# Loads of layer 1 issued by ScalarE instead of SyncE, with the first pass's row loads and normalisation spread over a strip

## The chip, the cores and the metric

The kernel runs on one core of a Trainium2 chip. The time is the device time of one execution in microseconds (us); it is 20,884.65 us as the median of three runs before the change (20,843.57 to 20,913.25). The engines are called as in the profile: PE (TensorE, matmuls; PEld is its weight load), DVE (VectorE), ACT (ScalarE), POOL (GpSimd), SP (SyncE, which here only issues DMAs). A name with a q (SPq, ACTq) is the instruction queue that issues DMAs. All data are 32-bit floats.

## The reference, cut to what matters

Four images of 48 channels and 256x256 pixels go through four residual layers, each `x = x + layer_n(norm(x))`, where `norm` takes mean and variance over groups of channels of an image. The change lies in layer 1 alone:

```
h = einsum('oc,bchw->bohw', w_in, norm(x))        # 48 -> 288 channels, 1x1
h = irfft2(rfft2(8x8 patches of h) * fft_mask)    # per channel a filter on each patch
h = conv3x3(h, depthwise, zero padding)           # per channel, across patch edges
x = x + einsum('oc,bchw->bohw', w_out, gelu(h[:144]) * h[144:])   # 144 -> 48
```

Layer 0 is of a like kind (Fourier products of patches), layer 2 samples an integral image at learned places (indirect DMAs on POOL), layer 3 is a gated network with a patch filter.

## The kernel before, in words

**Two streams.** The program is written as two generators whose steps are interleaved by due time: stream a runs layers 0 and 1 for image after image and then layer 3; stream b runs the first statistics, the weights of layer 1's filters (`patch_weights`) and layer 2. Each `yield n` adds n to the stream's own clock, and the stream that is behind goes next. So layer 1 of image 0 runs with nothing beside it, and layer 1 of images 1 to 3 runs beside layer 2 of the image before. `self.dma` (L227) issues on SP for stream a and on POOL for stream b; the column loads of layer 2 (`A<-x`, `B<-x`) are issued by ACT. A scheduler then puts the instructions of each engine in an order of its own, keeping the dependences, and buffers are handed out by pools (`hs`, `hg`, `ct` have two, `tt` three). PSUM gives stream a five banks (`self.bank()`). A DMA's landing is told by a completion semaphore; eight of them serve the DMAs of SP and ACT in turn.

**Layer 1, pass 1** (L690 to L710). An image is 16 strips of 16 rows (two halves of 8 rows, on partitions 0 to 47 and 64 to 111). `normalise(s)` takes a strip in four quarters of two rows: two loads (one for each half, 48 partitions x 516 floats, 96.8 KB) into one of two tiles `xn`, and a `tensor_scalar` on DVE (L684) that subtracts the mean, scales, and puts the rows as 8x8 patches into one of two tiles `xp`. The strip itself is 16 blocks b of two matmuls (L697, one for each half h): the block's pixels are the stationary operand, the weights `win` the moving one, and 288 channels come out in PSUM. The copy to the strip's tile `hs` is ACT's for h = 0 (L704) and DVE's for h = 1 (L702). After block 7 the whole of `normalise(s + 1)` is written. After block 15 one DMA writes `hs` (4,608 KB) to the scratch `hD` in HBM.

**Layer 1, pass 2** (L755 to L789). The 288 channels are 72 groups of four: c = 0, 1 of the gelu half, c = 2, 3 of the factor half. `fetch(g)` issues four loads: `hg` (1,024 KB, the group's patches from `hD`), `ct` (256 KB, the filter matrices), `tt` (256 KB) and `ht` (104 KB), the matrices of the 3x3 convolution within a patch and from the ring of pixels around it. Group g has four filter matmuls (L728), whose results are copied to `ys` by ACT (L734, even c) and DVE (L732, odd c). Eight DMAs (the list `AROUND`) then move the patches' edges from `ys` to the neighbours' ring `yh`. One group later `gated` takes the convolution as two matmuls for each c, from `ys` and `tt` (L741) and from `yh` and `ht` (L742), gelu on ACT (L745) and the product on DVE (L746) into `gt`; every second group one DMA writes `gt` to the scratch `gD` (1,024 KB). `fetch(g + 1)` is written ahead of group g's matmuls.

**Layer 1, pass 3** reads `gD` strip by strip, transposes and projects; the change doesn't touch it.

Of the kernel before, what the change touches and what calls it, by code (L numbers as in the profile page):

```python
# [11 lines left out]
ALU = mybir.AluOpType  # L12
# [7 lines left out]
NS = 16  # L20
# [6 lines left out]
NG = 72  # L27
# [12 lines left out]
NH = 52  # L40
# [148 lines left out]
class Net:  # L189
# [28 lines left out]
    def load(self, name, shape, pool=None):  # L218
        t = (pool or self.const).tile(shape, F32, name=name + "_sb", tag=name + "_sb")
        self.dma(t[:], self.a[name])  # L220
        return t
# [437 lines left out]
    def layer1(self, x, mr, y):  # L659
        nc, a = self.nc, self.a  # L660

        hD = self.dram.tile([128, NG, NS, 128], F32, name=self.nm("hD"))[:]
        gD = self.dram.tile([128, NS, NG // 2, 128], F32, name=self.nm("gD"))[:]
        with ExitStack() as ctx:
            w = ctx.enter_context(self.pool("wa", 1))
            sb = ctx.enter_context(self.pool("ba", 2))

            win = w.tile([112, 288], F32, name="win")
            mh = w.tile([112, 2], F32, name="mh")
            xns = [w.tile([112, 2, PW], F32, name=self.nm("xn")) for _ in range(2)]  # L670
            xps = [w.tile([112, 16, 128], F32, name=self.nm("xp")) for _ in range(2)]
            for t in xns:
                nc.vector.memset(t[32:64], 0.0)
            nc.vector.memset(mh[32:64], 0.0)
            for h in range(2):
                self.dma(win[64 * h : 64 * h + 48], a["L1_w_in"])
                self.dma(mh[64 * h : 64 * h + 48], mr[48 * h : 48 * h + 48])

            def normalise(s):

                for r in range(0, 8, 2):
                    xn = xns[r // 2 % 2]
                    self.load_rows(xn, x, 8 * s + r, 2, 64)
                    nc.vector.tensor_scalar(  # L684
                        xps[s % 2][:].rearrange("p b (r c) -> p r b c", c=16)[:, r : r + 2],
                        xn[:, :, 1:257].rearrange("p r (b c) -> p r b c", c=16),
                        mh[:, 0:1], mh[:, 1:2], ALU.subtract, ALU.mult,
                    )

            normalise(0)  # L690
            for s in range(NS):
                xp = xps[s % 2]
                hs = sb.tile([128, 4 * NG, 2, 16], F32, name="hs", tag="hs")
                for b in range(16):
                    for h in range(2):
                        ps = self.bank()
                        nc.tensor.matmul(  # L697
                            ps[:, :288], xp[64 * h : 64 * h + 48, b, :], win[64 * h : 64 * h + 48],
                            start=True, stop=True,
                        )  # L700
                        if h:
                            nc.vector.tensor_copy(hs[:, :, h, b], ps[:, :288])  # L702
                        else:
                            nc.scalar.copy(hs[:, :, h, b], ps[:, :288])  # L704
                    if b == 7:
                        if s + 1 < NS:
                            normalise(s + 1)
                        yield 13
                self.dma(hD[:, :, s, :], hs[:].rearrange("p (g c) h b -> p g (c h b)", c=4))
                yield 13  # L710
        with ExitStack() as ctx:
            w = ctx.enter_context(self.pool("wb", 1))
            sb = ctx.enter_context(self.pool("bb", 2))
            ys = [w.tile([128, YL], F32, name=self.nm("ys")) for _ in range(2)]
            yhs = [w.tile([NZ, YL], F32, name=self.nm("yh")) for _ in range(2)]
            hts = [w.tile([NZ, 4, 128], F32, name=self.nm("ht")) for _ in range(3)]
            for t in ys + yhs + hts:
                nc.vector.memset(t[:], 0.0)

            pick = lambda t, k, c: t[:k, Y0 + YC * c : Y0 + YC * c + 32 * YW].rearrange(  # L720
                "p (h s b) -> p s h b", h=2, b=YW
            )[:, :, :, :16]
            order = lambda t: t.rearrange("p (s h b) -> p s h b", h=2, b=16)
            todo, gt = None, None

            def filtered(c):
                ps = self.bank()
                nc.tensor.matmul(  # L728
                    ps[:].rearrange("p (s n) -> p s n", n=32), ct[:, c, :], hg[:, :, c, :], start=True, stop=True
                )  # L730
                if c % 2:
                    nc.vector.tensor_copy(pick(yt, 128, c), order(ps[:]))  # L732
                else:
                    nc.scalar.copy(pick(yt, 128, c), order(ps[:]))  # L734

            def gated(c):
                go, yo, yho, to, ho = todo
                both = []
                for q in (c, c + 2):
                    ps = self.bank()  # L740
                    nc.tensor.matmul(order(ps[:]), to[:, q, :], pick(yo, 128, q), start=True, stop=False)  # L741
                    nc.tensor.matmul(order(ps[:]), ho[:, q, :], pick(yho, NZ, q), start=False, stop=True)  # L742
                    both.append(ps)
                gl = sb.tile([128, 512], F32, name="gl", tag="gl")
                nc.scalar.activation(gl[:], both[0][:], AF.Gelu)  # L745
                nc.vector.tensor_mul(  # L746
                    gt[:, :, 2 * (go % 2) + c, :], gl[:].rearrange("p (s n) -> p s n", n=32),
                    both[1][:].rearrange("p (s n) -> p s n", n=32),
                )


            def fetch(g):
                hg = sb.tile([128, NS, 4, 32], F32, name="hg", tag="hg")
                self.dma(hg[:].rearrange("p s c n -> p s (c n)"), hD[:, g])
                ct = sb.tile([128, 4, 128], F32, name="ct", tag="ct")  # L755
                self.dma(ct[:], self.cD[g])
                tt = sb.tile([128, 4, 128], F32, name="tt", tag="tt", bufs=3)
                ht = hts[g % 3]
                tv = self.tD[4 * g : 4 * g + 4].rearrange("c (k m) -> k c m", m=128)
                self.dma(tt[:], tv[:128])  # L760
                self.dma(ht[:NH], tv[128:])
                return hg, ct, tt, ht

            fetched = {0: fetch(0)}
            for g in range(NG + 1):
                if g < NG:
                    yt = ys[g % 2]
                    if g + 1 < NG:
                        fetched[g + 1] = fetch(g + 1)
                    hg, ct, tt, ht = fetched.pop(g)  # L770
                if todo is not None and todo[0] % 2 == 0:
                    gt = sb.tile([128, NS, 4, 32], F32, name="gt", tag="gt")
                for c in range(2):
                    if g < NG:
                        filtered(2 * c)
                        filtered(2 * c + 1)
                    if todo is not None:
                        gated(c)
                if g < NG:
                    yh = yhs[g % 2]  # L780
                    n = YL - 2 * Y0
                    for k, m, p0, dp, far in AROUND:
                        self.dma(
                            yh[k : k + m, Y0 : Y0 + n], yt[p0 : p0 + (m - 1) * dp + 1 : dp, Y0 + far : Y0 + far + n]
                        )
                if todo is not None and todo[0] % 2:
                    self.dma(gD[:, :, todo[0] // 2, :], gt[:].rearrange("p s c n -> p s (c n)"))
                todo = (g, yt, yh, tt, ht)
                yield 12  # L789
# [582 lines left out]
```

## Time and profile before

| | |
|---|---|
| median of three runs | 20,884.65 us (20,843.57 to 20,913.25) |
| profiled execution, its own time | 20,882.08 us |
| its span in the profile | 20,880.3 us, mean granted TensorE clock 0.922 |
| busy: PE, DVE, POOL, ACT | 18,892.3, 10,763.0, 8,637.2, 5,909.3 us |
| chain of work that ended last | PE 65%, DMA 15%, DVE 7%, POOL 7%, "issue" 4%, SPq 1%, ACT 1% |
| pass 1 of images 0, 1, 2, 3 | 343, 543, 543, 542 us |
| pass 2 of images 0, 1, 2, 3 | 875, 1,142, 1,149, 1,130 us |
| pass 3 of images 0, 1, 2, 3 | 277, 280, 280, 279 us |

The stages are windows of the profiled execution: pass 1 from 1983, 5699, 9901 and 14107 us, pass 2 from 2351, 6269, 10471 and 14676 us. In a row of the costliest groups, the numbers behind the bar are the group's busy time, the mean of one instruction in ns, the idle time of the engine just before the group's instructions, and what ended most of that idle time. In a timeline a row is a start, a length, the engine and line, and in brackets the idle time before it with its releaser; a DMA row on SPq or ACTq is the time that its issue took, not the transfer.

### The profile page before, as it was taken

To read this page: it belongs to the slowest core of one execution; us is meant where nothing else is said; L and a number is where in the kernel's file an instruction comes from. 1 tells how busy PE (TensorE), PEld (TensorE's weight loads), DVE (VectorE), ACT (ScalarE), POOL (GpSimd) and SP (SyncE) were. 2 spreads that over 40 slices of the span, in tenths; PEclk is the share of its full clock that TensorE was granted. 3 is DMA by queue.
4 is the path that set the end of the run, shared out by engine and by line. 5 is a ranking of instruction groups with operands and counts; after the bars stand their busy time and mean duration, and the time that the engine had idled before them with its cause. 6 is when DMAs were issued, how large, how long until landed. Compare 5 with 4: busy or idle time off the path is not lost.

```text
span 20880.3 us, 231985 instructions
## 1 busy us (share of the span) xinstructions
PE 18892.3 (90%) x79032; PEld 12001.4 (57%) x79032; DVE 10763.0 (52%) x21931; ACT 5909.3 (28%) x12275; POOL 8637.2 (41%) x8887
## 2 busy tenths in 40 slices
PE   7998798999878989998788899997888999999999
PEld 4565435666533346665433466654334787878888
DVE  4544322477765534677645447776554255555521
ACT  2333312344321123443311234433112211111111
POOL 1000000277754511777555216775552066666600
PEclk9899799999968999999689899996899999999999
DMA  4623886555588975555889755558897566666633
GB/s 114 135 55 82 233 217 194 137 132 134 132 235 230 241 207 139 130 134 127 233 230 240 219 133 130 133 127 229 236 239 225 137 150 151 158 152 160 151 76 74
DMA packets 2444896, 3440.27 MB, mean 165 GB/s; under 512 B 580102, under 2 KB 1997038, under 8 KB 2333179
## 3 DMA queue, kind: packets, MB, share of 16 engines
q1 hardware_dynamic: 1908216, 2084.50, 38.2%
q0 software_dynamic: 452560, 1110.45, 21.1%
q10 hardware_dynamic: 82944, 230.48, 4.4%
q8 instruction: 635, 10.40, 0.2%
q14 instruction: 541, 4.43, 0.1%
HBM read 2486.99 MB, written 802.77 MB: 158 GB/s over the span
## 4 chain that ended last, share of the span: by engine, by line
PE 65%; DMA 15%; DVE 7%; POOL 7%; issue 4%; SPq 1%; ACT 1%; DVEq 0%; ACTq 0%; POOLq 0%
PE ps L427 19%; POOL V L1037 7%; PE ps L947 6%; PE ps L728 5%; PE ps L435 4%; PE ps L741 4%; DMA ct<-cD 4%; PE ps L742 3%; PE ps L697 3%; PE ps L828 3%; DMA hD<-hs 2%; PE ps L1188 2%; DVE V L1050 2%; PE ps L815 1%; PE ps L966 1%
## 5 line engine op out<-in xcount | busy, mean ns | idle before, releaser
L1037 POOL DMA_INDIRECT V<-t,idx x8192 | 8227.0, 1004 | 4897.9 <-issue 2346.8
L427 PE MATMUL ps<-W,A 128*128 128x288 f32 (+1 forms) x24576 | 5547.3, 374 | 85.9 <-DMA A<-x 23.4
L427 PEld LDWEIGHTS ps<-W,A 128*128 128x128 f32 x24576 | 4281.6, 191 | 1226.6 <-issue 523.4
L227 POOL DMA_DIRECT2D X<-x x192 | 144.5, 757 | 4302.6 <-DMA x<-xt 3040.1
L1050 DVE TENSOR_TENSOR V<-V 128x1536 f32<-128x1536 f32 (+3 forms) x2048 | 1839.3, 900 | 19.2
L1048 DVE TENSOR_TENSOR V<-V,w 128x3072 f32<-128x3072 f32 x512 | 1713.3, 3346 | 35.9 <-DMA V<-t,idx 27.0
L728 PE MATMUL ps<-hg,ct 128*128 128x512 f32 x2304 | 1264.4, 676 | 417.5 <-DMA ct<-cD 339.5
L947 PE MATMUL ps<-A,W 112*96 112x512 f32 x3072 | 1544.9, 642 | 26.2 <-DVE xt L1069 21.5
L697 PE MATMUL ps<-win,xp 48*128 48x288 f32 x4096 | 1054.8, 594 | 547.9 <-DVE xp L684 232.4
L508 ACT COPY qkv<-ps 128x288 f32<-128x288 f32 x2048 | 769.9, 400 | 2641.1 <-PE ps L427 1258.4
L435 PE MATMUL ps<-W,B 58*128 58x288 f32 (+1 forms) x8192 | 1271.5, 391 | 26.1 <-DMA B<-x 13.8
L742 PE MATMUL ps<-yh,ht 65*128 65x512 f32 x2304 | 1163.1, 649 | 145.7 <-DMA yh<-ys 111.6
L531 DVE BATCH_NORM_STATS2 bs<-ps 128x6 f32<-128x96 f32 x2048 | 397.4, 251 | 1634.3 <-PE ps L529 1632.3
L741 PE MATMUL ps<-ys,tt 128*128 128x512 f32 x2304 | 1174.1, 632 | 27.6 <-DVE ys L732 25.7
L697 PEld LDWEIGHTS ps<-win,xp 48*128 48x128 f32 x4096 | 647.3, 259 | 924.3 <-ACT hs L704 291.9
L1168 DVE TENSOR_TENSOR gp<-gl,ps 128x192 f32<-128x192 f32 x1024 | 353.8, 351 | 1588.1 <-ACT gl L1167 1579.9
L728 PEld LDWEIGHTS ps<-hg,ct 128*128 128x128 f32 x2304 | 468.0, 211 | 1051.6 <-issue 949.1
L1167 ACT ACTIVATE gl<-ps 128x192 f32<-128x192 f32 x1024 | 332.7, 330 | 2529.4 <-PE ps L427 2245.4
L435 PEld LDWEIGHTS ps<-W,B 58*128 58x128 f32 x8192 | 762.4, 186 | 454.1 <-issue 346.4
L746 DVE TENSOR_TENSOR gt<-gl,ps 128x512 f32<-128x512 f32 x576 | 395.1, 687 | 1142.2 <-PE ps L742 1136.6
L947 PEld LDWEIGHTS ps<-A,W 112*96 112x96 f32 x3072 | 513.9, 176 | 731.4 <-issue 690.3
L742 PEld LDWEIGHTS ps<-yh,ht 65*128 65x128 f32 x2304 | 451.3, 199 | 794.3 <-issue 699.4
(186 smaller groups left out, 24654.4 us busy)
## 6 DMA issues: line engine op xcount, KB each, us to landing
hD<-hs SPq DMA_DIRECT2D x64, 4608.0 KB
hg<-hD SPq DMA_DIRECT2D x288, 1024.0 KB
gD<-gt SPq DMA_DIRECT2D x144, 1024.0 KB
gs<-gD SPq DMA_DIRECT2D x64, 2304.0 KB
V<-t,idx POOLq DMA_INDIRECT x8192
A<-x SPq DMA_DIRECT2D x512, 193.5 KB
xt<-x SPq DMA_DIRECT2D x256, 387.0 KB
A<-x ACTq DMA_DIRECT2D x512, 193.5 KB
```

Source lines behind the costliest of these rows:

```text
L427: nc.tensor.matmul(to(q, b), A[:, r + q, 128 * b + g : 128 * b + g + 128], W[:, g, :], start=b == 0 and g == 0, stop=b == 1 and g == 2,)
L435: nc.tensor.matmul(to(q, b), B[p, r // 2, 128 * b : 128 * b + 128], W[p, 3, :], start=b == 1, stop=b == 0)
L508: nc.scalar.copy(t.qkv[:, 2 * q + b, :], banks[2 * b + q][:, 0:288])
L697: nc.tensor.matmul(ps[:, :288], xp[64 * h : 64 * h + 48, b, :], win[64 * h : 64 * h + 48], start=True, stop=True,)
L728: nc.tensor.matmul(ps[:].rearrange("p (s n) -> p s n", n=32), ct[:, c, :], hg[:, :, c, :], start=True, stop=True)
L741: nc.tensor.matmul(order(ps[:]), to[:, q, :], pick(yo, 128, q), start=True, stop=False)
L742: nc.tensor.matmul(order(ps[:]), ho[:, q, :], pick(yho, NZ, q), start=False, stop=True)
L828: nc.tensor.matmul(pp[:CP, :], pr[:, q, :], got[q][:], start=q == 0, stop=q == 2)
L947: m = nc.tensor.matmul(ps[:96, :].rearrange("p (r c) -> p r c", c=256), W[: kk[g], g, :], of[: kk[g]], start=g == 0, stop=g == 3,)
L1037: nc.gpsimd.indirect_dma_start(out=V[:, k, 4 * cr : 4 * cr + 4, :].rearrange("p e c -> p (e c)"), out_offset=None, in_=table, in_offset=ba ...
L1048: self.pinned(nc.vector.tensor_mul(Vm, Vm, wm.unsqueeze(2).to_broadcast([128, 64, 48])))
L1050: nc.vector.tensor_add(V[:, :, 0:n, :], V[:, :, 0:n, :], V[:, :, n : 2 * n, :])
```

## The change

In pass 1 the row loads are issued by ACT (`nc.scalar.dma_start`), and `normalise` is split into `load(s, n)` and `normalise(s, n)` for a quarter n. For the first strip the four pairs are written one after the other. For the others, the eight steps are written behind blocks 2, 4, 6, 7, 8, 9, 11 and 13 of the strip before, in the order of `plan`. In pass 2 the four loads of `fetch` are issued by ACT, and `fetch(g + 1)` is written behind group g's matmuls and gates (ahead of the `AROUND` DMAs) instead of ahead of them. The DMAs of `hD`, `AROUND` and `gD` stay on SP. From the end of the new lines on, line numbers of the changed kernel are 5 or 6 higher.

```
-            def normalise(s):
-
-                for r in range(0, 8, 2):
-                    xn = xns[r // 2 % 2]
-                    self.load_rows(xn, x, 8 * s + r, 2, 64)
-                    nc.vector.tensor_scalar(
-                        xps[s % 2][:].rearrange("p b (r c) -> p r b c", c=16)[:, r : r + 2],
-                        xn[:, :, 1:257].rearrange("p r (b c) -> p r b c", c=16),
-                        mh[:, 0:1], mh[:, 1:2], ALU.subtract, ALU.mult,
-                    )
-
-            normalise(0)
+
+            def load(s, n):
+                for h in range(2):
+                    nc.scalar.dma_start(xns[n % 2][64 * h : 64 * h + 48], self.rows(x, 128 * h + 8 * s + 2 * n, 2))
+
+            def normalise(s, n):
+                nc.vector.tensor_scalar(
+                    xps[s % 2][:].rearrange("p b (r c) -> p r b c", c=16)[:, 2 * n : 2 * n + 2],
+                    xns[n % 2][:, :, 1:257].rearrange("p r (b c) -> p r b c", c=16),
+                    mh[:, 0:1], mh[:, 1:2], ALU.subtract, ALU.mult,
+                )
+
+            for n in range(4):
+                load(0, n)
+                normalise(0, n)
+            plan = {2: (load, 0), 4: (load, 1), 6: (normalise, 0), 7: (load, 2), 8: (normalise, 1), 9: (load, 3),
+                    11: (normalise, 2), 13: (normalise, 3)}
...
+                    if b in plan and s + 1 < NS:
+                        do, n = plan[b]
+                        do(s + 1, n)
                     if b == 7:
-                        if s + 1 < NS:
-                            normalise(s + 1)
                         yield 13
...
             def fetch(g):
                 hg = sb.tile([128, NS, 4, 32], F32, name="hg", tag="hg")
-                self.dma(hg[:].rearrange("p s c n -> p s (c n)"), hD[:, g])
+                nc.scalar.dma_start(hg[:].rearrange("p s c n -> p s (c n)"), hD[:, g])
                 ct = sb.tile([128, 4, 128], F32, name="ct", tag="ct")
-                self.dma(ct[:], self.cD[g])
+                nc.scalar.dma_start(ct[:], self.cD[g])
...
-                self.dma(tt[:], tv[:128])
-                self.dma(ht[:NH], tv[128:])
+                nc.scalar.dma_start(tt[:], tv[:128])
+                nc.scalar.dma_start(ht[:NH], tv[128:])
...
             for g in range(NG + 1):
                 if g < NG:
                     yt = ys[g % 2]
-                    if g + 1 < NG:
-                        fetched[g + 1] = fetch(g + 1)
                     hg, ct, tt, ht = fetched.pop(g)
...
                     if todo is not None:
                         gated(c)
+                if g + 1 < NG:
+                    fetched[g + 1] = fetch(g + 1)
                 if g < NG:
                     yh = yhs[g % 2]
```

## The prediction

> **What bounds the kernel now.** I read the page's engine shares first, then its costliest groups for what PE (TensorE) waits for, then the windows by stage, and last the timeline inside one strip and one group.
>
> ```profile
> PE 18892.3 (90%) x79032; PEld 12001.4 (57%) x79032; DVE 10763.0 (52%) x21931; ACT 5909.3 (28%) x12275; POOL 8637.2 (41%) x8887
> ...
> L728 PE MATMUL ps<-hg,ct 128*128 128x512 f32 x2304 | 1264.4, 676 | 417.5 <-DMA ct<-cD 339.5
> ...
> L697 PE MATMUL ps<-win,xp 48*128 48x288 f32 x4096 | 1054.8, 594 | 547.9 <-DVE xp L684 232.4
> ...
> L742 PE MATMUL ps<-yh,ht 65*128 65x512 f32 x2304 | 1163.1, 649 | 145.7 <-DMA yh<-ys 111.6
> ```
>
> PE is busy 90% of the span, 1,988 us are idle, and the three matmul lines that the change feeds have 417.5 + 547.9 + 145.7 = 1,111 us of idle time ahead of them. The windows put that time in place; columns are length, busy PE, PEld, DVE, ACT, POOL, granted clock, DMA share, GB/s. The four lines are pass 1 and pass 2 of image 0, then of image 1.
>
> ```profile
> 1983.00:2326.00 343.00, 205.88 (x1024) 158.56 (x1024) 181.67 (x315) 153.35 (x256) 0.00 (x0) 0.67 0.86 240
> 2351.00:3226.00 875.00, 810.67 (x1701) 338.16 (x1702) 199.71 (x288) 171.62 (x285) 0.00 (x0) 0.93 0.80 216
> ...
> 5699.00:6242.00 543.00, 410.41 (x1360) 225.30 (x1360) 352.37 (x617) 170.09 (x276) 296.62 (x308) 0.64 0.80 229
> 6269.00:7411.00 1142.00, 1004.51 (x2317) 428.04 (x2317) 591.34 (x880) 192.55 (x317) 599.13 (x633) 0.90 0.91 237
> ```
>
> PE is idle 137 and 133 us in the two pass 1, 64 and 137 us in the two pass 2; images 2 and 3 repeat image 1 (132, 132; 145, 139). All of it: 1,019 us. But the DMA engines are busy 0.80 to 0.91 there. A stage can't become shorter than the larger of busy PE and DMA share x length: 295, 811, 434 and 1,039 us. So at most 48 + 64 + 3 x 109 + 320 = 759 us can be won. Why PE waits in pass 1 is seen in one strip's timeline (start, length, what; idle before in brackets):
>
> ```profile
> 2130.84 0.52 SPq L227 DMA_DIRECT2D hD<-hs  x1
> ...
> 2131.55 14.62 SPq L227 DMA_DIRECT2D xn<-x  x1
> ...
> 2133.47 1.81 PE L697 MATMUL ps<-win,xp 48*128 48x288 f32 x6 [11.00 <-DVE xp L684]
> ```
>
> SP issues the strip's hD write, and the next xn load, right behind it, takes 14.62 us to issue. The rows land late, L684 normalises late, and PE stands 11.00 us. In pass 2 SP's order is the matter:
>
> ```profile
> 2804.46 0.60 SPq L227 DMA_DIRECT2D gD<-gt  x1
> ...
> 2805.16 1.83 SPq L227 DMA_DIRECT2D hg<-hD  x1
> ...
> 2809.73 9.00 SPq L227 DMA_DIRECT2D yh<-ys  x8
> ...
> 2814.66 1.95 PE L728 MATMUL ps<-hg,ct 128*128 128x512 f32 x4 [2.28 <-DMA ct<-cD]
> ```
>
> The loads of the next group go out after the previous group's eight yh issues (9.0 us) and gD, some 9 us after their buffer was free in image 0 and 13.6 us in images 1 to 3; the filter matmul then waits 2.28 us.
>
> **What the Trainium skill says.** "DMA: Bandwidth & Descriptors", section Issuing engines are not separate DMA queues: starting DMAs from several engines saves only the sequencer's issuing time, "which is usually small". The trace disagrees on small: 14.62 us behind hD. Section Queues, rings and completion order of that page: each issuing engine has a ring of its own and the DMA engines go round between rings. So a load issued by ACT needn't stand behind hD's descriptors. The trace agrees as far as it shows it: ACT's A<-x issues take 0.3 to 1.5 us while an hD backlog lies on SP (5970 to 5976 us). Section Anatomy of one DMA: a wait on a semaphore is spent on the issuing sequencer. Here that means ACT, which has copies and gelus queued behind its loads. The waits by SP's queue show the same on SP: "<- DMA hD<-hs: 373.5" us in 22 times.
>
> **The change, part by part.** Only ACT and SP change in number: 1,664 DMAs (512 xn; 288 each of hg, ct, tt, ht) go from SP to ACT; POOL's queue, PE and DVE keep their counts. ACT's issuing time is 1,664 x 0.3 to 1.8 us; per group 1.83 + 1.17 + 0.60 + 0.59 = 4.2 us beside 172 / 73 = 2.4 us of work in a period of 12.0. That lies beside PE's work, 0 on the path as long as five PSUM banks cover a copy that stands behind one issue; without that cover up to 0.5 us a group.
>
> What counts is the wait before an issue. The built program hands eight completion semaphores in turn to all DMAs of SP and ACT, so each waits for the one eight places before it in program order. A strip of pass 1 has eight loads and one hD: nine. In image 0, in the built order, each strip's eighth load waits on ACT for hD of the strip before, and stands ahead of the ninth of ACT's 16 hs copies (L704). That wait was SP's before; now eight copies, and behind them PE through its banks, stand behind it. In images 1 to 3 the layer 2 column loads, already on ACT, shift the turn: such a wait falls ahead of copy 5 to 11 in 8 of 15 strips, and twice per image at a strip's end.
>
> *Pass 1, image 0.* The wait for xn goes (loads are issued a strip ahead). The period becomes hD's flight (18.3 to 19.3 us in this stage; estimate 20.7 with seven loads beside it), 0.5 us for the load, seven copies at PE's slow pace there (0.96 us a block: 6.7 us), 0.7 us to the next hD: 28.6 us against 22.55 (hD issues from 2017.24 to 2310.40, 13 strips). 13 x 6 = **+78 us**. Bounds: -48 (DMA floor above) to +110.
>
> *Pass 1, images 1 to 3.* A strip takes 34.5 us; copy 9 comes some 17 us after hD, whose flight is 22.2 us in the mean. Half of the strips wait some 5 us, the others no longer wait for SP: the chain gives hD 26.7% (145 us) and xn 7.7% (42 us) of this stage. I take -20 us each, **-60**; bounds -109 and +50 each.
>
> *Pass 2, image 0.* hg is issued when its buffer is free, so ct's wait ends, and SP's yh issues no longer stand behind 2805.16 to 2809.73. Late next is yh: c3's copy ends 2807.76, and 9.0 us of issues and 2 us of flight give 2818.8 against a next use at 2808.66 + 12.0 = 2820.7; but yh's semaphores now wait for hg, ct and ht of the group after next, which eats part of that lead. I take 12.0 to 11.3 us a group (PE alone: 811 / 73 = 11.1): **-50**; bounds -64 and +25.
>
> *Pass 2, images 1 to 3.* 1142 / 73 = 15.65 us, PE alone 13.8, DMA alone 0.91 x 15.65 = 14.2. With loads begun earlier the engines fill gaps, but transfers stay queued: 15.25, **-30 each, -90**; bounds -107 and +40 each.
>
> Sum: 78 - 60 - 50 - 90 = -122. The profiled execution took 20,882.08 us (span 20,880.3), 2.6 below the median of 20,884.65; 20,884.65 - 122 = **20,763 us**.
>
> **The rivals.** *A, the forecast (0.45)*: SP's backlog and lag are gone, part is paid back as hD's wait on ACT. Own range 20,640 to 20,870. *B, the large gain (0.20)*: ACT's wait for hD is covered by banks and by layer 2's PE work, and half of the 759 us comes: some 20,500. For it: PE waits on xn and ct in every strip and group. Against: in image 0 nothing else is there to do. *C, slower (0.22)*: ACT, held in order by landings, becomes the bound. It decides once hD lands later than ACT reaches the load ahead of copy 9: 18.3 us against 8 x 0.96 = 7.7 us in image 0 (certain there), 22.2 against 17 in images 1 to 3 (marginal). Price: +78, +1 us x 15 strips x 3 = +45, and in pass 2 tt and ht, waiting on ACT for yh or gD ahead of gelus, +0.5 us x 216 groups = +108: 21,115. *D, nothing (0.13)*: the change doesn't do what it says, because the DMA engines at 0.80 to 0.91 and the window of eight DMAs set both passes: 20,885.
>
> **How the numbers follow.** A measurement of this kernel can tell some 0.3%, 63 us, from no change: 20,822 to 20,947. Faster: 0.40 of A and B, 0.60. Same: 0.05 of A and 0.12 of D, 0.17. Slower: C and 0.01 of D, 0.23. From 20,500 (half of B lies below) to 21,000 (half of C above) no more than 0.2 is left out.
>
> **What would show it.** In the changed profile: L684's wait for xn (408.0 us) below 100; L728's wait for ct (339.5) below 100; the hs copies of ACT with some 13 waits of about 10 us for hD or xn in image 0; SP's wait for hD gone; the four windows near 421, 825, 523 and 1,112 us. I am wrong if pass 1 of image 0 is shorter than 343 us (no wait on ACT), if pass 2 is longer than before, or if PE waits for hs copies in images 1 to 3 more than the 270 us (151.3 by DVE, 118.8 by ACT) that L697 shows.

## The result, and the profile after

The changed kernel takes **21,721.69 us** (median of four runs, 21,703.06 to 21,728.49) against 20,886.03 us before: ratio 1.0401, 95% interval 1.0382 to 1.042. It is slower by 836 us; the forecast was 20,763, a gain. The profiled execution has a span of 21,701.0 us, 820.7 more than before. The page's rows that answer to those shown of before:

```profile
PE 19440.8 (90%) x79032; PEld 12205.1 (56%) x79032; DVE 10746.7 (50%) x21931; ACT 5915.1 (27%) x12275; POOL 8615.4 (40%) x8887
...
L748 PE MATMUL ps<-yh,ht 65*128 65x512 f32 x2304 | 1513.0, 816 | 725.1 <-DMA yh<-ys 526.9
...
L702 PE MATMUL ps<-win,xp 48*128 48x288 f32 x4096 | 1175.3, 627 | 532.4 <-ACT hs L709 382.6
...
L734 PE MATMUL ps<-hg,ct 128*128 128x512 f32 x2304 | 1231.7, 639 | 179.7 <-DMA ct<-cD 61.5
```

The wait that was aimed at did go: ct ends 61.5 us of the filter matmul's idle time instead of 339.5. In its place the ring's matmul (L748, L742 before) waits 526.9 us for `yh`, instead of 111.6. In pass 1 the wait for `xp` has become one for ACT's copies (382.6 us). The windows, same columns as before: pass 1 and pass 2 of image 0, then of image 1.

```profile
1983.00:2368.00 385.00, 260.25 (x1024) 191.19 (x1024) 181.39 (x317) 158.20 (x256) 0.00 (x0) 0.57 0.72 213
2394.00:3466.00 1072.00, 922.10 (x1701) 377.71 (x1702) 200.32 (x289) 171.73 (x285) 0.00 (x0) 0.84 0.63 177
5932.00:6495.00 563.00, 437.49 (x1360) 232.89 (x1360) 350.79 (x616) 169.15 (x276) 304.97 (x316) 0.63 0.76 223
6522.00:7828.00 1306.00, 1088.19 (x2318) 455.06 (x2319) 589.12 (x881) 192.51 (x317) 596.07 (x630) 0.83 0.80 207
```

By the first and last matmul of each stage (in pass 2, of its filter matmuls), pass 1 is longer by 41, 21, 14 and 20 us and pass 2 by 197, 163, 168 and 202 us: 95 + 729 = 824, all of the difference. Pass 3 has changed by 3 us at most. The DMA engines are less busy than before (0.63 for 0.80, 0.80 for 0.91), so it isn't bandwidth. In pass 2 of image 0 PE now stands ahead of the gates (L748) and hardly anywhere else: 35 times, 146 us in all.

```profile
PE ps L748 <- DMA tt<-tD: 92.3, 22, 4.7
PE ps L748 <- DMA yh<-ys: 50.0, 12, 5.6
PE ps L734 <- DMA ct<-cD: 30.3, 2, 26.6
PE ps L748 <- issue: 3.7, 1, 3.7
```

In these rows the numbers are us in all, times, and the longest. The waits by SP's queue in the same stage say where the lateness comes from; first before, then after:

```profile
SPq L227 <- DVE ys L732: 60.5, 36, 5.7
SPq L227 <- DMA tt<-tD: 48.5, 43, 2.2
SPq L227 <- PE ps L741: 45.6, 70, 1.7
SPq L227 <- DMA hg<-hD: 38.9, 34, 1.9
```

```profile
SPq L227 <- DMA hg<-hD: 331.4, 70, 7.8
SPq L227 <- DMA yh<-ys: 126.4, 97, 3.4
SPq L227 <- DMA ht<-tD: 96.4, 37, 5.9
```

SP no longer issues the loads, yet it waits for them more than before: 70 times 4.7 us for the landing of `hg`. What it has to issue then are the eight `AROUND` DMAs of a group, called the halo here. The reason lies in the built program: the eight completion semaphores are handed out in program order over both queues, and a DMA waits for the last one that held its semaphore. The trace's records of DMA issues carry the number: SP and ACT share semaphores 108 to 115, POOL has 99 to 106. With the loads on SP, each stood in SP's order behind the halo DMAs of the group before. On ACT they are begun right after the group's last copy, so their place in the turn is ahead of, and in the midst of, that group's own halo DMAs. A stretch of the changed kernel's timeline in pass 2 of image 0:

```profile
2898.25 27.27 SPq L227 DMA_DIRECT2D yh<-ys  x16
...
2899.95 6.81 PE L748 MATMUL ps<-yh,ht 65*128 65x512 f32 x8 [4.27 <-DMA tt<-tD]
...
2913.07 0.33 ACTq L760 DMA_DIRECT2D hg<-hD  x1
...
2915.51 3.73 PE L748 MATMUL ps<-yh,ht 65*128 65x512 f32 x8
...
2919.43 0.33 ACTq L767 DMA_DIRECT2D ht<-tD  x1
...
2930.28 4.74 PE L748 MATMUL ps<-yh,ht 65*128 65x512 f32 x6 [4.04 <-DMA tt<-tD]
```

Sixteen halo DMAs, two groups' worth, took 27.27 us to issue, 13.6 for a group's eight, against 9.00 before. (A group's gates are four matmuls in the program and eight records here.) The single issues and landings in the trace show what the second eight waited for:

- The first halo DMA has the semaphore of `hg`. `hg` was begun at 2913.07, when its buffer was free, and landed at 2917.83; the halo DMA went out at 2917.91.
- The sixth and seventh have the semaphores of the second and third, because the loads have used up places of the turn. They went out at 2922.82 and 2924.04, 0.02 us after those had landed.
- The eighth has that of `ht`, whose buffer is free only after the gates of the group before (2915.51 and 3.73 us). `ht` was begun at 2919.43 and landed at 2924.39, in time for the eighth at 2924.80.
- The eighth landed at 2930.04, and the next gates start at 2930.28. It was 5.2 us in flight, beside `hg` and `ct` of the next group (begun at 2923.64 and 2923.99). The eighth of the group before, without such company, took 2.0 (2909.74 to 2911.78).

The tag "DMA tt<-tD" on the last row names another transfer that landed then; in the program L748 waits for the eight halo DMAs.

The stage alternates. In every second group PE waits at the gates, 4.1 us in the mean, and the steps are those above: of 34 such groups the first halo DMA was held by `hg` in 33, a later one by its own group's landings in 33, the eighth by `ht` in 3. In the groups between, `ht` does hold the seventh halo DMA (in 33 of 36), but the gates find their halo in place, because PE is slow there: after the pause eight records of L748 took 6.81 us, without one 3.73. A period that ends in a wait is 14.9 us in the mean and one without it 15.3, where PE's busy time before was 811 / 73 = 11.1 a group.

It is still a loop, over two groups: gates that start late, PE's matmuls behind them, the buffer that they free, `hg`, the halo, gates.

### The profile page after: what moved, and what is told of

Its sections match the earlier page's. It is cut to its first block, busy times and chain, and to the rows that moved or that the text cites. A ratio compares the mean times of both kernels' runs of the same rounds, so it can differ in the third digit from the quotient of the medians.

```text
span 21701.0 us, 230822 instructions
## 1 busy us (share of the span) xinstructions
PE 19440.8 (90%) x79032; PEld 12205.1 (56%) x79032; DVE 10746.7 (50%) x21931; ACT 5915.1 (27%) x12275; POOL 8615.4 (40%) x8887
## 3 DMA queue, kind: packets, MB, share of 16 engines
q1 hardware_dynamic: 1576792, 1550.02, 28.6%
## 4 chain that ended last, share of the span: by engine, by line
PE 66%; DMA 17%; DVE 6%; POOL 6%; issue 3%; ACT 1%; SPq 1%; ACTq 0%; DVEq 0%; POOLq 0%
PE ps L427 20%; PE ps L953 6%; PE ps L748 6%; POOL V L1043 6%; PE ps L435 4%; DMA hD<-hs 4%; DMA yh<-ys 4%; PE ps L734 3%; PE ps L747 3%; PE ps L834 3%; PE ps L702 2%; PE ps L1194 2%; DMA tt<-tD 2%; PE ps L891 1%; DVE V L1056 1%
## 5 line engine op out<-in xcount | busy, mean ns | idle before, releaser
L748 PE MATMUL ps<-yh,ht 65*128 65x512 f32 x2304 | 1513.0, 816 | 725.1 <-DMA yh<-ys 526.9
L702 PE MATMUL ps<-win,xp 48*128 48x288 f32 x4096 | 1175.3, 627 | 532.4 <-ACT hs L709 382.6
L953 PE MATMUL ps<-A,W 112*96 112x512 f32 x3072 | 1626.2, 671 | 10.3 <-DVE xt L1075 5.6
L748 PEld LDWEIGHTS ps<-yh,ht 65*128 65x128 f32 x2304 | 556.3, 248 | 1552.3 <-issue 1214.7
L734 PE MATMUL ps<-hg,ct 128*128 128x512 f32 x2304 | 1231.7, 639 | 179.7 <-DMA ct<-cD 61.5
L702 PEld LDWEIGHTS ps<-win,xp 48*128 48x128 f32 x4096 | 698.2, 273 | 972.4 <-ACT hs L709 607.7
L740 ACT COPY ys<-ps 128x512 f32<-128x512 f32 x576 | 347.2, 603 | 3021.1 <-PE ps L734 1619.2
```

Source lines behind the costliest of these rows:

```text
L702: nc.tensor.matmul(ps[:, :288], xp[64 * h : 64 * h + 48, b, :], win[64 * h : 64 * h + 48], start=True, stop=True,)
L734: nc.tensor.matmul(ps[:].rearrange("p (s n) -> p s n", n=32), ct[:, c, :], hg[:, :, c, :], start=True, stop=True)
L953: m = nc.tensor.matmul(ps[:96, :].rearrange("p (r c) -> p r c", c=256), W[: kk[g], g, :], of[: kk[g]], start=g == 0, stop=g == 3,)
```

## The experiments

Two theories stood against the **loop** (halo DMAs held by the landing of later loads): **contention** (loads now fly beside the halo DMAs and slow them) and **ACT's blocked queue** (rival C). The runs come from several chips. On three of them every kernel, the one before included, takes 25.0 to 25.7 ms, with longer stages where layer 2 runs beside; why is open. Image 0's stages agree across all chips (before's pass 1: 340 to 343 us), so stage times are compared in image 0 or on one chip.

**p1only**: the change's pass 1, the pass 2 of before.

> The change's pass 1 with the pass 2 of before. If the two passes lose time each for itself: the 95 us that the windows of pass 1 show (41 + 21 + 14 + 20) stay and pass 2 is as before, some 20,980 us, windows near 384, 563, 556, 562 and 875, 1142, 1149, 1130. If pass 1's new loads are what slows pass 2 (clock or queue carried over), pass 2 keeps part of its 729 us: 21,200 or more.

Measured: 20,972.02 us, ratio 1.0043 (1.0029 to 1.0058). Pass 1 took 385, 554, 558 and 560 us; pass 2 took 866, 1,133, 1,123 and 1,130.

**p2only**: the pass 1 of before, the change's pass 2.

> The pass 1 of before with the change's pass 2. If the passes are independent: 20,885 + 729 = some 21,615 us, pass 2 near 1072, 1305, 1316, 1331. If they are not, the loss is well below 700 us.

Measured: 21,619.93 us, ratio 1.0355 (1.0334 to 1.0376); pass 2 took 1,066, 1,323, 1,327 and 1,318 us, pass 1 as before. The two losses nearly add up: 78 us of p1only and 726 of p2only make 803 of the 836. No run moves `fetch` in the source alone, with its DMAs on SP; that this part changes nothing is not shown. With the halo on POOL it makes no difference where `fetch` stands (p2_yh_pool and best, below: 790 and 789 us).

**p2_hg**: on top of p2only, ct, tt and ht back on SP; hg stays on ACT.

```
-                nc.scalar.dma_start(ct[:], self.cD[g])
+                self.dma(ct[:], self.cD[g])
...
```

> Pass 1 of before; in pass 2 only hg is issued by ACT, ct, tt and ht stay on SP. Loop theory (the halo DMAs wait, through the completion semaphores, for the landing of ct, tt and ht of a later group; ht waits for the gates before): the loop is cut, since these three again stand behind the halo DMAs in SP's order, and pass 2 is near before or better: 840 to 890 us in image 0, 1,100 to 1,150 in the others. Contention theory (hg, 1 MB, now flies beside the halo DMAs and slows them): most of the loss stays, over 1,000 and over 1,250. Theory of ACT's blocked queue: a quarter of the issues, a quarter of the loss: 920 and 1,185.

Measured: ratio 1.0218 (1.0197 to 1.0239); pass 2 took 1,052, 1,234, 1,217 and 1,225 us. My own number for the loop theory (840 to 890) failed. The waits of SP's queue in image 0 show how:

```profile
SPq L227 <- DMA hg<-hD: 320.6, 36, 11.2
SPq L227 <- PE ps L742: 22.8, 15, 4.7
```

In this order `ht` shares hg's semaphore and stands on SP ahead of a group's halo DMAs, so half of the groups wait some 9 us for `hg`. The wait has moved by one DMA and the halo is held all the same. In images 1 to 3 about half of the loss has gone. By itself image 0's time (over 1,000) would also fit contention.

**p2_yh_pool**: on top of p2only, the halo on POOL, whose DMAs have semaphores of their own.

```
-                        self.dma(
+                        nc.gpsimd.dma_start(
                             yh[k : k + m, Y0 : Y0 + n], yt[p0 : p0 + (m - 1) * dp + 1 : dp, Y0 + far : Y0 + far + n]
```

> Pass 1 of before; pass 2 of the change, but the eight halo DMAs are issued by POOL, whose DMAs have completion semaphores of their own. To be read in image 0, where POOL has no other work (in images 1 to 3 they stand behind gathers). Loop theory: yh no longer waits for the landing of loads, pass 2 of image 0 goes from 1,072 to 860 to 930 us. Contention theory and the theory of ACT's blocked queue: it stays over 1,030.

Measured: ratio 1.0249 (1.0225 to 1.0273) for the whole, but **790 us** in image 0's pass 2, below before's 875.

```profile
2349.00:3139.00 790.00, 768.59 (x1700) 321.82 (x1701) 200.00 (x288) 171.75 (x285) 295.69 (x568) 0.98 1.02 240
```

```profile
2806.13 0.33 ACTq L754 DMA_DIRECT2D hg<-hD  x1
...
2807.41 4.17 POOL L783 DMA_DIRECT2D yh<-ys  x8 [4.26 <-issue]
...
2808.57 3.73 PE L742 MATMUL ps<-yh,ht 65*128 65x512 f32 x8
```

The first fence is the window of the stage, the second its timeline: the eight halo DMAs go out in 4.17 us right beside `hg`. They take 7.8 to 9.4 us to land, and cost nothing. PE is busy 97% at a granted clock of 0.98. SP's queue still waits for `hg`, but only `gD` stands behind that wait:

```profile
SPq L227 <- DMA hg<-hD: 442.6, 34, 44.2
```

So loads that fly beside the halo don't make the loss by themselves, and neither does ACT's issuing of them. By the issue records, ACT's loads waited 102 us in this stage, nearly all for PE to free a buffer. In the change it was 146 us, 27 of them for landings, most of them of ACT's own `tt`. That holds for image 0. The run gives the halo other semaphores, another queue and a shorter issue (4.17 us for eight) at once; that the semaphores held it is read from SP's waits, not separated by this run. In images 1 to 3 the halo shares POOL with layer 2's gathers: its first DMA went out 4.1 to 4.4 us after the group's last copy in the mean, against 0.6 in image 0, and pass 2 took 1,326 to 1,334 us, as in p2only.

**p2_nocorner** and **b_nocorner**: the change's pass 2, and the kernel before, each with four of the eight halo DMAs left out.

```
-                    for k, m, p0, dp, far in AROUND:
+                    for k, m, p0, dp, far in AROUND[:4]:
```

> Pass 1 of before, pass 2 of the change, with the four one-partition corner DMAs of the halo left out (their part of the result is not computed): four loads and four halo DMAs a group, so that the eight semaphores come round once a group and a halo DMA waits for DMAs of the group before, not for loads begun after its own data were ready. If the turn of the semaphores makes the loop, it is gone in all four images: 790 to 850 and 1,050 to 1,140 us. If it is ACT's blocked queue or the contention of loads and halo, most of the loss stays: over 1,000 and over 1,250.

> The kernel before with the same four corner DMAs left out, as the yardstick of the run above: four issues of 0.75 us less on SP for each group. 840 to 870 us in image 0 and 1,080 to 1,140 in the others if SP's issue order is what delays ct there; unchanged if the engines' share (0.91) is.

Measured (one chip): p2_nocorner 938.7 us in image 0 and 1,288, 1,287, 1,287 in the others; b_nocorner 821.1 and 1,289, 1,323, 1,294. The number for image 0 (790 to 850) failed, and so did the rivals' (over 1,000): with gD in the turn it doesn't come round evenly, and SP still waits 190.3 us for `hg` in image 0. The two go together: the wait fell from 331.4 to 190.3 us (by 43%) and the loss from 197 to 939 - 821 = 118 us (by 40%). In images 1 to 3 the times are over the rivals' 1,250, but so are the yardstick's: no loss is left against it, though ACT issues every load. On such a chip there is less to lose, as the next pair shows. b_nocorner itself is 54 us below before's 875 in image 0, more than expected: the halo cost time in the kernel before too.

**p2_noht** and **p2only_b** (one chip): the loads of `ht` taken out, and the yardstick.

```
-                nc.scalar.dma_start(ht[:NH], tv[128:])
+                if g < 3:
+                    nc.scalar.dma_start(ht[:NH], tv[128:])
```

> Pass 1 of before, pass 2 of the change, but ht is loaded for the first three groups alone and those matrices are used for all (the ring's part of the convolution is computed with wrong matrices). It takes one edge out of the loop: gates of the group before -> ht begun by ACT -> landing -> eighth halo DMA -> landing -> gates. The other edge, first halo DMA waits for hg's landing, stays. If the ht edge closes the loop of 14.9 us a group: 840 to 940 us in image 0. If hg's landing alone does: over 1,030.

> The change's pass 2 with the pass 1 of before once more, as the yardstick on the chip of the run beside it: 1,066 us in image 0, as before. In images 1 to 3, if this chip is one where layer 2's gathers run slower and pass 2 of before takes 1,360 to 1,420: the loop theory says that the loop is not lengthened by that, so the loss against before is smaller than 163 to 201 us; if the loss is a slowed engine or contention, it is as large or larger.

Measured: 1,005 us for p2_noht, 1,069 for p2only_b in image 0. Neither number of the expectation was met: leaving out `ht` is worth 64 of some 195 us, a third. It also takes one DMA out of each group's turn, and in the change `ht` held the halo mostly in groups whose gates didn't wait, so the third can't be put down to the ht edge alone.

SP's waits in the first 937 us of that stage:

```profile
SPq L227 <- DMA hg<-hD: 399.9, 65, 10.8
SPq L227 <- DMA gD<-gt: 49.2, 32, 2.4
```

SP's wait for `hg` is still 399.9 us there. That the larger part of the loss is the first halo DMA, and SP's queue behind it, held until `hg` has landed, fits this; no run has that edge alone taken out. In images 1 to 3 p2only_b took 1,421, 1,415 and 1,422 us, p2_noht 1,371, 1,355 and 1,361, 49 to 60 us less. How much p2only_b loses there is seen from the totals on that chip: 25,664.95 us against 25,375.82 before (ratio 1.0112, 1.0083 to 1.0142), 289 us. Image 0's pass 2 accounts for some 200 of them (1,069 against 866 to 875 elsewhere), which leaves some 30 us for each other image (an estimate; 4 to 54 by the interval), and not 163 to 202: where the stage is slow for another reason, the loop is mostly covered.

**p1_3rows** and **p1_3rows_sp**: pass 1 with seven DMAs a strip instead of nine, issued by ACT or by SP; pass 2 of before.

```
-            xns = [w.tile([112, 2, PW], F32, name=self.nm("xn")) for _ in range(2)]
+            xns = [w.tile([112, 3, PW], F32, name=self.nm("xn")) for _ in range(2)]
...
+            ROWS = (3, 3, 2)
...
+            plan = {2: (load, 0), 4: (load, 1), 6: (normalise, 0), 7: (load, 2), 9: (normalise, 1), 12: (normalise, 2)}
```

> The change's pass 1 (loads by ACT), but a strip is loaded in three pieces of 3, 3 and 2 rows instead of four of 2: six loads and one hD make seven DMAs a strip for eight semaphores, so in image 0 no load waits for hD any more. Pass 2 as before. If hD's wait on ACT, ahead of the ninth copy, makes pass 1 of image 0 longer: its 384 us fall below before's 343, to 300 to 335 (DMA share 0.86 x 343 = 295). If the early loads themselves do it (they fly beside hD), it stays at 375 or more. Images 1 to 3 keep some of these waits through layer 2's column loads: 530 to 560 each.

> As the run with three pieces, but the loads are issued by SP, spread over the strip as in the change. If the issuing engine is what matters in images 1 to 3 (a wait on SP holds only DMAs, one on ACT holds copies): 520 to 540 us each, below the ACT version. In image 0, SP issues the loads behind hD's descriptors again (14.6 us in one case): near the ACT version if the loads go out ahead of hD, else 330 to 345.

Measured: ratios 0.9967 (0.9955 to 0.9979) and 0.9978 (0.9967 to 0.999). Image 0's pass 1 takes 290.9 us with ACT, below the 300 to 335 expected, and 361.1 with SP, above its 330 to 345; before 343.4, the change 384.4. The change's wait in this stage, a case of it in the timeline, and the window of p1_3rows:

```profile
ACT hs L709 <- DMA hD<-hs: 119.5, 14, 9.9
```

```profile
2122.93 0.31 ACTq L682 DMA_DIRECT2D xn<-x  x1
2123.28 1.63 ACT L709 COPY hs<-ps 128x288 f32<-128x288 f32 x3 [8.50 <-DMA hD<-hs]
```

```profile
1983.00:2274.00 291.00, 241.44 (x1024) 182.76 (x1024) 179.74 (x301) 159.21 (x256) 0.00 (x0) 0.64 0.95 280
```

The load at 2122.93 waits for hD (issued 2104.5) on ACT, and the ninth copy behind it starts 8.50 us late. With seven DMAs on eight semaphores ACT's waits for hD shrink from 119.5 us to 18.8, and the DMA engines are 0.95 busy. That the pieces are fewer and larger is not enough: with SP they are the same, and there L689 waits 148.8 us for xn, as L684 does in the kernel before. In images 1 to 3 the order turns round: 645, 643, 641 us with ACT and 621, 633, 617 with SP, where the pass 1 of before took 637 to 660 on that chip: ACT is the worse place there; that it is because copies stand behind a held load, and layer 2's column loads take part in the turn, is argued from the order and not shown by a run.

**best** and **c_halo0**: put together from these runs. The loads of pass 1 come in three pieces as above; c_halo0 has the first and the last edit alone.

```
+        alone = x is self.x[0]
...
+                    (nc.scalar.dma_start if alone else self.dma)(
+                        xns[n % 2][64 * h : 64 * h + 48, : ROWS[n]], self.rows(x, 128 * h + 8 * s + 3 * n, ROWS[n])
+                    )
...
+                start = nc.scalar.dma_start if alone else self.dma
+                start(hg[:].rearrange("p s c n -> p s (c n)"), hD[:, g])
...
-                        self.dma(
+                        (nc.gpsimd.dma_start if alone else self.dma)(
                             yh[k : k + m, Y0 : Y0 + n], yt[p0 : p0 + (m - 1) * dp + 1 : dp, Y0 + far : Y0 + far + n]
```

> A version put together from the runs: image 0 (nothing beside it) has the loads of pass 1 in three pieces on ACT, the fetch of pass 2 on ACT and the halo DMAs on POOL; images 1 to 3 have the loads of pass 1 in three pieces on SP, spread over the strip, and the pass 2 of before. If the gains add up: 52 (pass 1, image 0: 291 for 343) + 85 (pass 2, image 0: 790 for 875) + 3 x 15 to 28 (pass 1, images 1 to 3) = 180 to 220 us less than before, ratio 0.989 to 0.992. If the gains in images 1 to 3 belong to the slower chip alone: 137 us, 0.9935.

> The kernel before, with only the halo DMAs of image 0 issued by POOL; the fetch stays on SP. If in the run with halo on POOL the separation of halo and loads is the whole gain, whichever engine issues the loads: pass 2 of image 0 near 790, some 85 us less than before. If the early loads from ACT are needed for it: 830 to 860, and 15 to 45 us less.

Measured: best 25,438.79 us against 25,674.92 before on that chip, 236 us less, ratio **0.9905** (0.9887 to 0.9922); c_halo0 ratio 0.9968 (0.9947 to 0.9989). Image 0's pass 2 is 789 us in both, so putting the halo on POOL is the whole gain there, and which engine issues the loads then doesn't matter. It takes the halo out of the loads' turn and its issues off SP, ahead of the loads, at once; which of the two helps the kernel before is not separated. Image 0's pass 1 in best is 291 us; images 1 to 3 take 632, 632 and 627 in pass 1, against 659, 663 and 655 in c_halo0, whose pass 1 is that of before: 27 to 31 us an image, where 15 to 28 were expected. Best is faster than before on one chip; the change, measured on another, is slower than before by a ratio of 1.0401.

## Why the prediction was wrong

- **What bounds the kernel** held: PE's waits in the two passes were for xn and ct, and both shrank: ct's to 61.5 us, below 100 as said, L685's for xn from 408.0 to 212.5, which is not below 100. SP's wait for hD went from 373.5 to 21.5 us, as said.
- **Pass 2, image 0** (-50 forecast, +197 measured) is the step that failed, and images 1 to 3 (-90 forecast, +532 measured) with it. The prediction saw the wait, "yh's semaphores now wait for hg, ct and ht of the group after next", and priced it as "part of that lead" of 2 us. It should have been followed as a chain: hg's flight of 4.8 us ahead of the first halo DMA, the issues of the later ones held by landings in their own group, and the eighth's flight of 5.2 us, where 2 were counted, ahead of the gates. In place of 11.3 us a group the measured period is 14.9: PE waits 4.1 us for the halo in every second group, and in the other its matmuls take longer, which the prediction had put at nothing.
- **Rival C** was the right side with, in image 0, the wrong queue. It put the price on ACT (0.5 us a group for tt and ht, waiting for yh or gD ahead of gelus; 21,115 us). ACT's four loads waited for yh or gD only 3 us in all there, and 3 to 15 us in each other image. The wait that the Trainium skill describes ("DMA: Bandwidth & Descriptors", section Anatomy of one DMA: spent on the issuing sequencer) fell on SP, 331.4 us for hg in image 0 against 38.9. There it holds the halo, worth 197 / 72 = 2.7 us a group in image 0 and 2.3 to 2.8 in the others.
- **Pass 1, image 0** (+78 forecast, +41 measured): the mechanism was right, its size was not. hD's flight is 18.4 us beside seven loads (2104.5 to 2122.9), as without them, where 20.7 was assumed, and from there to the next hD at 2129.9 it is 7.0 us, not 7.9. The period is 25.4 us here and 25.9 in the mean of twelve strips, not 28.6.
- **Pass 1, images 1 to 3** (-20 forecast, +21, +14, +20 measured): the gain from SP's lag was counted, ACT's held copies too little. PE's wait for ACT's copies went from 118.8 to 382.6 us, of which image 0 has some 99. The prediction had named a rise there as its sign of error. PE's idle time itself did not grow (133 us before, 126 after in image 1): what grew is its busy time, 410.4 to 437.5 us for the same matmuls. That ACT's held copies are the cause is argued; the pair p1_3rows and p1_3rows_sp, where ACT is 10 to 24 us an image slower than SP, fits it.
- **The bound of 811 us** for pass 2 of image 0 was not one: 790 and 789 us were reached, since PE's busy time fell to 768.6 us, with fewer pauses.

What stays open: the cause of images 1 to 3's loss in pass 2 on the first chip, and how much belongs to each edge. That it is the same wait is seen in the trace (SP waits 1,034.6 us for hg over the whole run, 206.9 before), not shown by an experiment there: p2_yh_pool kept the loss in these images, p2_hg took about half of it away, and contention is not excluded by either.

## What to carry to other kernels

In a program built like this one, moving a DMA to another queue also moves its place in the turn of the completion semaphores, and a DMA that stays behind can inherit its landing as a wait. So count the DMAs between two that share a semaphore, on both queues together, and follow the wait until the chain ends or comes back to its start. A small DMA that something waits for soon should not share a turn with large loads: a queue with semaphores of its own (pass 2 of image 0), or fewer DMAs per period than there are semaphores (pass 1 of image 0), was worth more here than issuing the loads earlier.

## What was not expected of the hardware

PE's busy time for the same 1,700 matmul records of image 0's pass 2 goes with the pauses: 768.6 us at a granted clock of 0.98, 810.7 at 0.93, 922.1 at 0.84. A new wait was paid twice: of the 197 us, 111 are busy PE and 86 idle. And halo DMAs that took some 8 to 9 us to land beside 1 MB loads cost nothing, while ones that landed in 2 to 6 us but were issued late cost 197 us.
